# Two fused attention blocks on one core: the first norm's averages one quarter earlier in a weight product, and layer 0's bias products behind the second Q and K

## The chip, the cores and the metric

The kernel runs on one core of one Trainium2 chip. The metric is device time in microseconds (us) of the whole program, median over several executions. The core's engines work side by side, each through its own queue in order: TensorE (PE, matmuls; PEld is its weight load), VectorE (DVE), ScalarE (ACT), GpSimd (POOL), and SyncE (SP), which here issues nearly all DMAs. Line numbers (L504) are those of the kernel as the profile names them.

## The reference, cut to what matters

Input x is (8, 512, 32, 32), float32: 8 samples of 512 channels and 1024 positions. Two attention blocks with residuals follow each other.

```python
# layer 0: group norm (32 groups), 8 heads of 64
h = group_norm(x, norm_w, norm_b)
q, k, v = heads(einsum('oc,bchw->bohw', qkv_w, h) + qkv_b)
attn = softmax(einsum('bhnd,bhmd->bhnm', q, k) / sqrt(64))
o = einsum('bhnm,bhmd->bhnd', attn, v)
x = x + einsum('oc,bchw->bohw', proj_w, o) + proj_b

# layer 1: norm over the whole sample, one head of 512
n = (x - mean) * rsqrt(var + 1e-5) * gn_gamma + gn_beta
q, k, v = wq @ n + bq, wk @ n + bk, wv @ n + bv
attn = softmax(q^T k / sqrt(512))
x = x + wo @ (v attn^T) + bo
```

Since the rows of a softmax sum to one, the bias of V goes through attention unchanged. Layer 0's V bias can therefore be multiplied with the projection weights once (`proj_w @ bv + proj_b`) and be added behind the projection; the kernel does that, and the like for layer 1.

## The kernel before

**Tiling.** A sample is four tiles of 128 partitions x 1024 floats, each tile two channel chunks of one half of the positions. All matmuls are float32, and each shows in the profile as two records. Projections use a Strassen scheme (`strassen`, with seven products in place of eight): its weights come in parts A11, A12, A22 and a rest (A21), and four sums S1 to S4 that `Weight.finish` makes on VectorE (L182 to L185) and then stores to DRAM for the later samples (L220). The data side has the sums T1 to T4 (`Combined.first` and `second`). The products A11 x B11 and A12 x B21 come first and need no sum.

**Order.** TensorE, ScalarE and VectorE run in the order in which the program writes their instructions. `strassen` is a generator that yields between products; `together` interleaves several of them, and `at_steps` counts the yields and runs hooks after given ones. The second Q and K of layer 0 (`pairs_qk(w, 1, ...)`: channel chunks 1 and 3) make ten yields, 0 to 9, even for Q, odd for K. At step 8 Q's last two products (A22 x T4 and S4 x B22) are issued, at step 9 K's. SP's queue is not written by hand: the framework orders its DMAs and hands out the tile buffers.

**Buffers.** Most SBUF tiles (x, q, k, v, p, sums, `many`, `row`) come from one pool of 36. Three weight buffers rotate. PSUM has two tags, "s" and "o", of two buffers each; a buffer is two banks. `strassen` takes one "s" buffer and one "o" buffer, and leaves the second bank of the "o" one as `spare[0]`, in which the small averages of the norms are made (`room`).

**Start of the program.** First come the statistics of sample 0; the product of layer 1's V and output weights (`product(wvo1, ...)`, 16 matmuls of 512 columns); then the product of layer 1's Q and K weights (`wqk1`), in four quarters over `cc` of four matmuls each. `product` runs the callbacks of `between` behind the second and the fourth matmul of its last quarter: `norm.mean_of_all` (a small matmul at L268, then VectorE L272 to L312) and `norm.variance_of_all` (a matmul, VectorE, a power on GpSimd at L318, VectorE L326 to L328). Behind the product come two `Through` objects (bias1 and bias_q1): each copies a column of the vectors to 32-column blocks (`many`, L500, VectorE) and makes four matmuls with 32 weight columns each, one column group per channel chunk (L504). Then `norm.normed` (L336 on ScalarE, L338 on VectorE), `taken` (ScalarE copies of the finished product, L545 and L546), and the first Q and K of layer 0.

**Seam of sample 0.** In `layer0`, after V (L453, done at L485 and L487) the program adds up the two biases, finishes the weights qk13 and p0 and makes `Through` bias0 from p0's parts:

```python
        w = next_weight()
        if b == 0:
            w.finish()
            waiting[0].finish()
            p0 = waiting[0]
            ...
            throughs[:] = [Through(moving, V_BV0, V_BP0, "bias0", banks("s", "ps_bias0")[:, 0, :])]
            throughs[0].store()
            throughs[0].fetch()
```

`store` copies the row on ScalarE (L508) and issues four small DMAs (L511), `fetch` four more (L516); `add`, behind all of layer 0's scores, adds them up. Then the second Q and K run (L438; ScalarE copies L385, VectorE additions L470, ScalarE L468), with the next sample's norm in hooks 4 to 7 and the first scores (`score`, L626) in hooks 8 and 9.

Of the kernel before, what the change touches and what calls it, by code (L numbers as in the profile page):

```python
# [40 lines left out]
P = 128  # L41
C = 512
NC = C // P
# [16 lines left out]
def two_attention_blocks(  # L60
# [17 lines left out]
    nc = tc.nc  # L78
# [13 lines left out]
    def banks(tag, name):  # L92
        return psum.tile([P, 2, HALF], FP, tag=tag, name=name)

    def tile2(name):
        return tpool.tile([P, 2, HALF], FP, tag="t", name=name)
# [93 lines left out]
    class Weight:  # L190
# [3 lines left out]
        def __init__(self, name):  # L194
            self.name, (self.src, self.widths) = name, SOURCES[name]
            self.tile = wpool.tile([P, W_SIZE], FP, tag="w", name=f"w_{name}")
            self.parts, self.rest, at = [], [], 0
            for width in self.widths:
                size = len(A_PARTS) * 2 * width
                self.parts.append(parts_of(self.tile[:, at : at + size], width))  # L200
                at += size
            if name in stored:
                nc.sync.dma_start(self.tile, stored[name])
# [29 lines left out]
    waiting = []  # L233
# [191 lines left out]
    def at_steps(steps, hooks):  # L425

        n = -1
        for n, _ in enumerate(steps):
            for hook in hooks.get(n, []):
                hook()  # L430
        assert n >= max(hooks, default=-1)
# [44 lines left out]
    def make_v(w, n2, bs, vs, name):  # L476
# [11 lines left out]

        return strassen(by_positions(w, n2, bs), done, f"{name}_{n2}")

    class Through:

        def __init__(self, moving, v_bias, bias, name, ps):
            self.bias, self.name, self.ps = bias, name, ps
            many = tile2(f"many_{name}")[:, 0, :P].rearrange("p (c m) -> p c m", c=NC)
            at = vec[:, v_bias : v_bias + NC]
            nc.vector.tensor_copy(many, at.unsqueeze(2).to_broadcast([P, NC, P // NC]))  # L500
            for cc in range(NC):
                for to, w in moving(cc):
                    rows = ps[cc * (P // NC) : (cc + 1) * (P // NC), to]
                    nc.tensor.matmul(rows, many[:, cc, :], w, start=True, stop=True)  # L504
# [23 lines left out]
    def product(w, a, b, tag, between=()):  # L528


        w.rest = [tile2(f"rest_{w.name}")[:, :, : 2 * P]]
        ps = [banks(tag, f"ps_{w.name}_{j}") for j in range(2)]
        between = list(between)
        for cc in range(NC):
            for to in range(NC):
                nc.tensor.matmul(  # L536
                    ps[to // 2][:, to % 2, :], a[cc][:, to * P : (to + 1) * P], b[cc],
                    start=cc == 0, stop=cc == NC - 1,
                )
                if cc == NC - 1 and to % 2 and between:  # L540
                    between.pop(0)()

        def taken():
            for j in range(2):
                nc.scalar.copy(w.parts[0][f"A1{j + 1}"], ps[j][:, :, : 2 * P])  # L545
                nc.scalar.copy(w.parts[0]["A22"] if j else w.rest[0], ps[j][:, :, 2 * P :])  # L546

        return taken
# [49 lines left out]
    def layer0(bs, qs, ks, b, load_next, norm_next):  # L598
# [69 lines left out]
        ps = {}  # L668
# [4 lines left out]
        w = next_weight()  # L673
        if b == 0:
            w.finish()
            waiting[0].finish()
            p0 = waiting[0]

            def moving(cc):
                for i in range(2):  # L680
                    a = p0.rest[0] if (i, cc // 2) == (1, 0) else p0.parts[0][f"A{i + 1}{cc // 2 + 1}"]
                    yield slice(i * 2 * P, (i + 1) * 2 * P), a[:, cc % 2, :]

            throughs[:] = [Through(moving, V_BV0, V_BP0, "bias0", banks("s", "ps_bias0")[:, 0, :])]
            throughs[0].store()
            throughs[0].fetch()
        hooks = {8: [lambda: score(0)], 9: [lambda: score(1)]}
        *pairs, end = ORDER
        if norm_next is not None:
            hooks[4] = [lambda: norm_next().mean_of_all()]  # L690
            hooks[5] = [lambda: norm_next().variance_of_all()]
            combine = Combined(f"0_{b + 1}")
            for half in range(2):
                hooks[6 + half] = [lambda half=half: norm_next().normed(norm_next().xs, [half])]
            hooks[8].insert(0, lambda: combine.first(norm_next().xs))
            hooks[9].insert(0, combine.second)
            bs_next = combine.parts
        at_steps(together(*pairs_qk(w, 1, bs, qs, ks, b)), hooks)
        xs = load_x(b, nc.sync)
        norm = norm1(xs, b)  # L700
# [243 lines left out]
    with tc.manual_schedule(engines={PE, ACT, DVE}):  # L944
        norm = norm0(xs_next, 0)
        for cc in range(NC):
            norm.of_half(cc, 0)
        for cc in range(NC):
            norm.of_half(cc, 1)
            norm.of_channels(cc)  # L950
        wvo1 = Weight("wvo1")
        product(wvo1, nv1, wo1, "o")()
        waiting.append(load_first("qk02"))
        wqk1 = Weight("wqk1")
        wvo1.finish()
        spare[0] = banks("o", "ps_norm")[:, 0, :]
        taken = product(wqk1, nq1, nk1, "s", [norm.mean_of_all, norm.variance_of_all])
        spare[0] = None
        ps = banks("o", "ps_biases")
        everywhere = slice(0, C)  # L960
        throughs += [
            Through(lambda cc: [(everywhere, wo1[cc])], V_BV1, V_BO1, "bias1", ps[:, 0, :]),
            Through(lambda cc: [(everywhere, nk1[cc])], V_BQ1, None, "bias_q1", ps[:, 1, :]),
        ]
        norm.normed(xs_next)
        taken()
        waiting.append(load_first("v0"))
        for through in throughs:
            through.store()
        combine = Combined("0_0")  # L970
        combine.first(xs_next)
        waiting[0].finish()
        combine.second()
        bs = combine.parts
        qs, ks = [None] * NC, [None] * NC
        w = next_weight()
        at_steps(
            together(*pairs_qk(w, 0, bs, qs, ks, 0)), {2: [wqk1.finish], 8: [waiting[0].finish]}
        )
        for through in throughs:  # L980
            through.fetch()
        for b in range(B):
            ahead = []

            def load_next():
                ahead.append(norm0(load_x(b + 1, nc.sync), b + 1))

            norm_next = (lambda: ahead[0]) if b + 1 < B else None
            xs, norm, bs = layer0(bs, qs, ks, b, load_next, norm_next)

            qs, ks = [None] * NC, [None] * NC
            hs, combine = quarters_of(f"h_1_{b}"), Combined(f"1_{b}")
            steps = [
                norm.mean_of_all, norm.variance_of_all, lambda: norm.normed(hs, [0]),
                lambda: norm.normed(hs, [1]), lambda: combine.first(hs), combine.second,
            ]
            if b + 1 < B:
                at_steps(
                    together(*pairs_qk(next_weight(), 0, bs, qs, ks, b + 1)),
                    {n + 4: [step] for n, step in enumerate(steps)},  # L1000
                )
            else:
                for step in steps:
                    step()
            at_values = {}
            if b + 1 < B:

                again, combine_next = ahead[0], Combined(f"again_{b}")

                def load_again():  # L1010
                    again.xs = load_x(b + 1, nc.sync)

                at_values = {
                    2: [load_again], 5: [lambda: again.normed(again.xs, [0])],
                    6: [lambda: again.normed(again.xs, [1])], 8: [lambda: combine_next.first(again.xs)], 9: [combine_next.second],
                }
                bs = combine_next.parts
            attention1(xs, combine.parts, b, at_values)
            for half in range(2):
                for i in range(2):  # L1020
                    nc.sync.dma_start(quarter_of(out, b, i, half), xs[i][half])


        assert next(extents, None) is None
        good = small.tile([P, 1], FP, tag="good", name="good")
        nc.vector.tensor_reduce(good, extent, AX.X, ALU.add)
        nc.vector.tensor_scalar(good, good, MOST, None, ALU.is_le)
        ps = banks("o", "ps_good")[:, 0, :]
        nc.tensor.matmul(ps[:, 0:1], ones, good, start=True, stop=True)
        nc.vector.tensor_copy(flag, ps[0:1, 0:1])  # L1030
# [412 lines left out]
```

## Time and profile before

| | us |
|---|---|
| median of 9 runs | 2953.09 |
| lowest, highest | 2951.51, 2954.72 |
| profiled execution, time | 2953.3 |
| profiled execution, span from first to last instruction | 2951.6 |
| mean granted TensorE clock | 0.995 |
| TensorE busy | 2916.4 |
| VectorE busy | 1753.7 |
| ScalarE busy | 1070.8 |

The profile is one execution of the program. In the timeline a row gives the start, the length, the engine, the line, the operation with its tiles (out<-in, buffer numbers left out), how many instructions are merged in it, and in brackets the idle time of the engine ahead of it with what ended it. "issue" means that no releaser is seen. The lengths of matmuls include their pipeline, so rows overlap a little.

### The profile page before, as it was taken

To read this page: it belongs to the slowest core of one execution; us is meant where nothing else is said; L and a number is where in the kernel's file an instruction comes from. 1 tells how busy PE (TensorE), PEld (TensorE's weight loads), DVE (VectorE), ACT (ScalarE), POOL (GpSimd) and SP (SyncE) were. 2 spreads that over 40 slices of the span, in tenths; PEclk is the share of its full clock that TensorE was granted. 3 is DMA by queue.
4 is the path that set the end of the run, shared out by engine and by line. 5 is a ranking of instruction groups with operands and counts; after the bars stand their busy time and mean duration, and the time that the engine had idled before them with its cause. 6 is when DMAs were issued, how large, how long until landed. Compare 5 with 4: busy or idle time off the path is not lost.

```text
span 2951.6 us, 33920 instructions
## 1 busy us (share of the span) xinstructions
PE 2916.4 (99%) x14018; PEld 1359.1 (46%) x14018; DVE 1753.7 (59%) x2142; ACT 1070.8 (36%) x1512; POOL 13.9 (0%) x26
## 2 busy tenths in 40 slices
PE   9999999999999999999999999999999999999898
PEld 4434545345543455334553354533545335453353
DVE  4577265862658536684366844578445783547835
ACT  2363224622146221562215522165222642226321
POOL 0000000000000000000000000000000000000000
PEclk9999999999999999999999999999999999999999
DMA  7301122011220112202031021310212212120001
GB/s 252 148 15 45 62 66 106 23 50 50 93 79 23 50 50 93 86 15 75 26 118 62 15 75 34 109 62 15 75 61 82 69 33 75 43 91 24 8 0 37
DMA packets 63402, 184.27 MB, mean 62 GB/s; under 512 B 13308, under 2 KB 13820, under 8 KB 56840
## 3 DMA queue, kind: packets, MB, share of 16 engines
q1 hardware_dynamic: 63096, 182.01, 18.0%
q8 instruction: 112, 1.84, 0.3%
q14 instruction: 50, 0.41, 0.0%
q10 hardware_dynamic: 144, 0.02, 0.0%
HBM read 137.41 MB, written 27.81 MB: 56 GB/s over the span
## 4 chain that ended last, share of the span: by engine, by line
PE 95%; DVE 4%; ACT 1%; issue 0%; SPq 0%; DMA 0%; POOL 0%; DVEq 0%; POOLq 0%
PE s L626 15%; PE ps_o L645 14%; PE ps_q L438 13%; PE ps_v L453 13%; PE ps_o L893 13%; PE ps_s L836 13%; PE ps_k L438 7%; PE ps_p L438 4%; DVE inv L566 1%; PE ps_sum L659 1%; DVE acc L555 1%; PE ps_wvo L536 1%; PE ps_wqk L536 0%; DVE t_p L711 0%; DVE t_p L705 0%
## 5 line engine op out<-in xcount | busy, mean ns | idle before, releaser
L553 ACT ACTIVATE p<-s 128x1024 f32<-128x1024 f32 x512 | 523.8, 1025 | 314.7 <-PE s L626 311.3
L626 PE MATMUL s<-q,k 64*64 64x512 f32 x4096 | 532.6, 591 | 0.0
L645 PE MATMUL ps_o<-p,v 64*64 64x512 f32 x4096 | 528.7, 589 | 0.0
L555 DVE TENSOR_TENSOR acc<-acc,p 128x1024 f32<-128x1024 f32 x384 | 468.7, 1220 | 80.7 <-ACT p L553 63.7
L626 PEld LDWEIGHTS s<-q,k 64*64 64x64 f32 x4096 | 151.9, 133 | 295.1 <-issue 254.0
L645 PEld LDWEIGHTS ps_o<-p,v 64*64 64x64 f32 x4096 | 156.6, 133 | 282.8 <-issue 280.3
L844 DVE TENSOR_TENSOR p<-ps_s,u_s 128x512 f32<-128x512 f32 x96 | 66.4, 692 | 249.7 <-ACT u_s L385 139.4
L487 DVE TENSOR_TENSOR v<-ps_v,u_v 128x512 f32<-128x512 f32 x96 | 66.3, 690 | 201.4 <-PE ps_v L453 130.5
L385 ACT COPY u_v<-ps_v 128x512 f32<-128x512 f32 x96 | 56.3, 586 | 326.3 <-PE ps_v L453 320.0
L385 ACT COPY u_q<-ps_q 128x512 f32<-128x512 f32 x96 | 56.3, 586 | 317.5 <-PE ps_q L438 317.4
L836 PE MATMUL ps_s<-s_q,t 128*128 128x512 f32 x384 | 167.4, 592 | 0.0
L893 PE MATMUL ps_o<-t_p,s_v 128*128 128x512 f32 x384 | 166.1, 592 | 0.0
L555 DVE TENSOR_TENSOR acc<-p,p 128x1024 f32<-128x1024 f32 x64 | 78.4, 1225 | 98.9 <-ACT p L553 98.9
L438 PE MATMUL ps_p<-t_p,w_p 128*128 128x512 f32 x256 | 113.3, 595 | 4.5 <-DVE inv L566 4.5
L470 DVE SCALAR_TENSOR_TENSOR q<-ps_q,bias_q,u_q 128x512 f32<-128x512 f32 x48 | 36.0, 751 | 137.2 <-ACT u_q L385 74.8
L836 PEld LDWEIGHTS ps_s<-s_q,t 128*128 128x128 f32 x384 | 73.0, 190 | 91.8 <-issue 91.8
L893 PEld LDWEIGHTS ps_o<-t_p,s_v 128*128 128x128 f32 x384 | 73.0, 190 | 91.8 <-issue 88.5
L893 PE MATMUL ps_o<-p,v 128*128 128x512 f32 x256 | 113.3, 595 | 0.0
L453 PE MATMUL ps_v<-w_wvo,t 128*128 128x256 f32 x512 | 113.1, 379 | 0.0
L836 PE MATMUL ps_s<-q,h 128*128 128x512 f32 x256 | 112.5, 592 | 0.0
L438 PE MATMUL ps_q<-t,w_wqk 128*128 128x512 f32 x256 | 112.5, 592 | 0.0
L566 DVE RECIPROCAL inv<-ps_sum 128x512 f32<-128x512 f32 x32 | 107.4, 3356 | 7.1 <-ACT held_sum L562 7.1
(208 smaller groups left out, 3601.0 us busy)
## 6 DMA issues: line engine op xcount, KB each, us to landing
x<-in_x SPq DMA_DIRECT2D x92, 512.0 KB
w_qk<-stored_qk SPq DMA_DIRECT2D x14, 1792.0 KB
out<-x SPq DMA_DIRECT2D x32, 512.0 KB
w_wqk<-stored_wqk SPq DMA_DIRECT2D x8, 1792.0 KB
w_wvo<-stored_wvo SPq DMA_DIRECT2D x8, 1792.0 KB
w_v<-stored_v SPq DMA_DIRECT2D x7, 1792.0 KB
w_p<-stored_p SPq DMA_DIRECT2D x7, 1792.0 KB
inv<-inv SPq DMA_DIRECT2D x192, 64.0 KB
```

Source lines behind the costliest of these rows:

```text
L385: nc.scalar.copy(us[n], line)
L438: nc.tensor.matmul(bank, w[a][:, k, c * P : (c + 1) * P], bs[b][:, k, :], start=fresh and k == 0, stop=k == 1, skip_group_check=True,)
L453: nc.tensor.matmul(bank[:, u * 2 * P : (u + 1) * 2 * P], bs[b][:, k, n * P : (n + 1) * P], w[a][:, k, :], start=fresh and u == k == 0, sto ...
L487: nc.vector.tensor_tensor(v, pairs(bank), pairs(u), ALU.add)
L553: nc.scalar.activation(p, s, AF.Exp, scale=factor)
L555: nc.vector.tensor_tensor(acc, first, p, ALU.add)
L566: nc.vector.reciprocal(inv, ps)
L626: nc.tensor.matmul(s[cols, j, :], flat(ks[pair])[rows, k0 : k0 + HD], qs[pair][rows, g, :], start=True, stop=True,)
L645: nc.tensor.matmul(o[cols, half, :], vs[kt][rows, c0 : c0 + HD], p[rows, j, :], start=kt == 0, stop=kt == NT - 1,)
L836: nc.tensor.matmul(bank, bs[b][:, k, t * P : (t + 1) * P], q_parts[a][:, k, :], start=fresh and k == 0, stop=k == 1, skip_group_check=True,)
L844: nc.vector.tensor_tensor(p, bank, u, ALU.add)
L893: nc.tensor.matmul(bank, v_parts[kt // 2][a][:, kt % 2, c * P : (c + 1) * P], p_parts[kt // 2][b][:, kt % 2, :], start=fresh and kt == 0, ...
```

## The change

Three things. In `product`, the callbacks run in the last quarter but one (`cc == NC - 2`) in place of the last. The copy to `many` becomes a function of its own, and for bias1 and bias_q1 it is called ahead of the product. For sample 0, `p0.finish` moves into hook 7 of the second Q and K (behind the second half of the next sample's normalisation), and the products, store and fetch of bias0 become the first thing in hook 8, ahead of `combine.first` and of the first scores; the products are written to the spare bank in place of an "s" buffer.

```diff
+    def many(v_bias, name):
+        t = tile2(f"many_{name}")[:, 0, :P].rearrange("p (c m) -> p c m", c=NC)
+        at = vec[:, v_bias : v_bias + NC]
+        nc.vector.tensor_copy(t, at.unsqueeze(2).to_broadcast([P, NC, P // NC]))
+        return t
...
-        def __init__(self, moving, v_bias, bias, name, ps):
+        def __init__(self, moving, many, bias, name, ps):
             self.bias, self.name, self.ps = bias, name, ps
-            many = tile2(f"many_{name}")[:, 0, :P].rearrange("p (c m) -> p c m", c=NC)
-            at = vec[:, v_bias : v_bias + NC]
-            nc.vector.tensor_copy(many, at.unsqueeze(2).to_broadcast([P, NC, P // NC]))
...
-                if cc == NC - 1 and to % 2 and between:
+                if cc == NC - 2 and to % 2 and between:
                     between.pop(0)()
...
         if b == 0:
             w.finish()
-            waiting[0].finish()
             p0 = waiting[0]
...
-            throughs[:] = [Through(moving, V_BV0, V_BP0, "bias0", banks("s", "ps_bias0")[:, 0, :])]
-            throughs[0].store()
-            throughs[0].fetch()
+            def bias0():
+                throughs[:] = [Through(moving, many(V_BV0, "bias0"), V_BP0, "bias0", room("bias0"))]
+                throughs[0].store()
+                throughs[0].fetch()
...
+        if b == 0:
+            hooks.setdefault(7, []).append(p0.finish)
+            hooks[8].insert(0, bias0)
         at_steps(together(*pairs_qk(w, 1, bs, qs, ks, b)), hooks)
...
+        manys = [many(V_BV1, "bias1"), many(V_BQ1, "bias_q1")]
         taken = product(wqk1, nq1, nk1, "s", [norm.mean_of_all, norm.variance_of_all])
...
-            Through(lambda cc: [(everywhere, wo1[cc])], V_BV1, V_BO1, "bias1", ps[:, 0, :]),
-            Through(lambda cc: [(everywhere, nk1[cc])], V_BQ1, None, "bias_q1", ps[:, 1, :]),
+            Through(lambda cc: [(everywhere, wo1[cc])], manys[0], V_BO1, "bias1", ps[:, 0, :]),
+            Through(lambda cc: [(everywhere, nk1[cc])], manys[1], None, "bias_q1", ps[:, 1, :]),
```

## The prediction

> **What bounds the kernel now.** I read the page first, then TensorE's own waits over the whole run, and then the timeline of the two places that those waits point to. The page says that TensorE sets the time:
>
> ```profile
> PE 2916.4 (99%) x14018; PEld 1359.1 (46%) x14018; DVE 1753.7 (59%) x2142; ACT 1070.8 (36%) x1512; POOL 13.9 (0%) x26
> ```
>
> The span is 2951.6 us, so TensorE is idle for about 35 us in all, and an edit that adds or removes no matmul can only gain from these or from a slow clock. The waits of TensorE name where some of them lie (columns: total us, times, longest us):
>
> ```profile
> PE ps_bias L504 <- issue: 7.2, 1, 7.2
> ...
> PE ps_biases L504 <- DVE many_bias_q L500: 2.4, 1, 2.4
> ...
> PE ps_q L438 <- ACT rest_wqk L546: 0.3, 1, 0.3
> ```
>
> All three lie where the change edits. The timeline of the first place (start us, length us, engine, line, what, and the idle time before it):
>
> ```profile
> 33.12 0.28 PE L268 MATMUL ps_norm<-stat,in_group 128*128 128x4 f32 x2
> 35.06 0.28 PE L268 MATMUL ps_norm<-spread,in_group 128*128 128x4 f32 x2
> 35.89 1.01 POOL L318 TENSOR_TENSOR rstd<-rstd,minus_half 128x4 f32<-128x4 f32 x1 [33.88 <-DVE rstd L317]
> 37.53 2.93 ACT L336 ACTIVATE x<-x,shift,scale 128x512 f32<-128x512 f32 x4 [15.16 <-DVE shift L328]
> 37.78 1.94 PE L504 MATMUL ps_biases<-wo,many_bias 128*32 128x512 f32 x8 [2.44 <-DVE many_bias_q L500]
> 41.46 3.70 PE L438 MATMUL ps_q<-x,w_qk 128*128 128x512 f32 x8 [0.32 <-ACT rest_wqk L546]
> ```
>
> The product of layer 1's weights ends with the variance matmul at 35.06. Its answer goes through VectorE, GpSimd and VectorE to the shift, ScalarE normalises from 37.53 (four activations, 2.93 us), and then copies ps_wqk out of the PSUM buffer that the first Q needs (copies at 40.37 and 40.83). So Q starts at 41.46, and what ended last is ScalarE's chain from the shift; the bias products between (37.78 to about 41.1) end just ahead of it. The statistics were ready long before, at 19.4 (aggregate at 19.17 for 0.21).
>
> The second place is the seam between batch 0's V and its second Q and K:
>
> ```profile
> 96.19 0.68 DVE L185 TENSOR_TENSOR w_p<-w_p 128x512 f32<-128x512 f32 x1
> 96.80 0.22 DVE L500 COPY many_bias<-vec 128x128 f32<-128x128 f32 x1
> 97.12 1.10 PE L504 MATMUL ps_bias<-w_p,many_bias 128*32 128x256 f32 x8 [7.18 <-issue]
> ...
> 99.00 5.25 PE L438 MATMUL ps_q<-x,w_qk 128*128 128x512 f32 x8
> ...
> 104.10 3.60 PE L438 MATMUL ps_k<-x,w_qk 128*128 128x512 f32 x8
> ```
>
> V's products end at 89.94 (chain of waits: "65.76 24.17"). TensorE then stands for 7.18 us. The releaser reads "issue", but the first bias product reads `many_bias`, which VectorE writes at 96.80 after the last V addition, five small additions, eight operations of qk13's finish and four of p0's. Behind it, eight records of Q take 5.25 us where K's eight take 3.60: the clock. The granted clock by the microsecond (columns: stretch, sum; PE, PEld, DVE, ACT, POOL busy; PEclk; DMA share; GB/s):
>
> ```profile
> 37.00:38.00 1.00, 0.22 (x4) 0.23 (x8) 0.93 (x6) 0.47 (x1) 0.00 (x0) 0.66 0.00 0
> ...
> 96.00:97.00 1.00, 0.00 (x0) 0.00 (x0) 1.00 (x3) 0.00 (x0) 0.00 (x0) 0.50 1.01 430
> ...
> 103.00:104.00 1.00, 1.00 (x3) 0.38 (x3) 0.00 (x0) 0.17 (x1) 0.00 (x0) 1.00 0.99 416
> ```
>
> **The change, part by part.** All sums are against the profiled execution: span 2951.6 us, time 2953.3, of which 1.7 lies outside the span. The median of the nine runs, 2953.09, is 0.2 below it.
>
> *Averages in the third quarter.* The weight product is 32 records of 0.43 us, 8 to a quarter. The mean matmul follows the 20th record in place of the 28th, the variance the 24th in place of the 32nd: each 8 x 0.43 = 3.43 us earlier, at 29.7 and 31.6. VectorE has been idle since 25.0 (idle of 8.41 before the mean's copy), and needs 1.07 us from the mean matmul to the finished spread (33.12 to 34.19) where 1.9 are there, so neither stalls the product. The shift and ScalarE's start move from 37.53 to 34.10. ScalarE's last-quarter inputs are there: ps_wqk's first buffer is complete about 33.4, its second at 35.3, both before the copies at 36.9. Q moves to 41.46 - 3.43 = 38.03.
>
> *`many` for bias1 and bias_q1 ahead of the product.* Two VectorE copies of 0.22 us go into the idle stretch from 25.0: nothing on the path. The 16 bias products no longer wait for them and follow the product at once, at 35.3. They run in four column groups, four records together: 0.84 us for four at clock 0.50 (37.78 to 41.1), thus 0.43 at full clock, 1.7 us, over at 37.0. They are under the ScalarE chain by 1 us. If they ran at the old pace, 3.36 us, they would end at 38.7 and be the bound; the gain would be 2.8. I take 3.4, since the clock read 1.00 until 37.3 and the array is now busy up to 37.0. **First place: -3.4 (bounds -2.8 and -3.4).** Everything up to the seam follows the Q start and moves along.
>
> *Nothing ahead of the second Q and K.* The bias0 products leave, and with them the wait. The first Q product reads A11 of qk13, which needs no finish, and batch 0's normalised x; DMA share is 0.00 from about 78 to 90, so the weights have landed. Its PSUM buffers are those that V's first half gave back (copy at 84.79, addition at 86.52). Q's eight records end 3.43 us after V, K's eight at 6.86. In old times: 89.94, 93.37, 96.80. VectorE finishes qk13 at 94.3, adds q by 95.0, and Q's S1 product needs both at 96.80: covered by 1.8 us. Gone are 99.08 - 89.94 = 9.14 us, and 5.18 - 3.43 = 1.75 us of half clock in the first Q: -10.9.
>
> *What comes back at the end of the second Q and K.* p0.finish is now in VectorE's queue after the second half of the next sample's normalisation (step 7), and bias0 stands in TensorE's queue between Q's last product and the first scores (step 8). The old rows there:
>
> ```profile
> 119.94 0.99 DVE L338 TENSOR_SCALAR x<-x,scale,shift 128x512 f32<-128x512 f32 x2
> ...
> 121.80 1.09 PE L626 MATMUL s<-q,k 64*64 64x512 f32 x8
> 121.91 0.75 DVE L470 SCALAR_TENSOR_TENSOR q<-ps_q,vec,u_q 128x512 f32<-128x512 f32 x1 [0.98 <-PE ps_q L438]
> ```
>
> VectorE had 0.98 us free before Q's last addition. Now four operations come in at 120.87, and took 96.80 - 94.26 = 2.54 us at the seam: free at 123.4. Then q's addition (0.67 to the next start) and `many` at 124.1; the products start 0.32 after it (96.80 to 97.12), at 124.4. TensorE is there at 121.8: **a new stall of 2.6 us**, with the scores, the rest of K and all else queued behind it. The 16 products of 256 columns took 1.96 us at clock 0.50, thus 1.0 at full clock. ScalarE's row copy (0.59) stands ahead of the first exponential, which waits for the scores anyway; combine.first, 2.4 us on VectorE, is for the next sample and late for nobody: k's last addition follows K's products, some 3.6 us further on. Cost: +3.6.
>
> *DMAs.* The store of p0 (1.79 MB), four stores of 2 KB and four fetches leave the seam, where DMA share was about 1.0, and go on SP's queue after qk13's store and about the load of wqk1 and the reload of x (126.55 and 126.94). Their readers are far: bias0 is added at 242.5, the x reload is read at 253. Bounds 0 and, if a tile has to wait for the row's store, the 8 us from row copy to last fetch at the seam (99.14 to 107.1); I take 0.
>
> *The clock at the new stall* is the open term. The row: at the first place TensorE was idle from 35.3, and the clock fell to half near 37.3, 2.0 us later (0.66 in 37 to 38), though only 2.44 us were idle. At the seam it fell near 95.3, 5.4 us after V. The Trainium skill ("TensorE: Matmul & The Clock Gate", Part 1: The HAM clock gate) says that the array is throttled after at least one idle window of about 3.4 us, that the windows run free, and that a busy one lifts it. By the idle-window rule a stall of 2.6 us costs no clock: the sum is -3.4 - 10.9 + 3.6 = -10.7. By the row of 2.44 us it may: a window of 3.4 us at half speed loses 1.7, and the sum is -9.0. The row overrides the word "idle": a window that was partly busy was enough. But clock edges at 37.3, 40.7, 95.3 and 102.2 fit one grid of 3.41 us, as the page has it. On it the new stall, at 121.8 - 14.3 = 107.5 to 110.1, is cut by an edge at 109.0: the window before it is busy for 1.9 of 3.4 us, against 1.4 in the one that lost the clock. I take full clock, and keep the other end for the range.
>
> **Sum.** -3.4 - 10.9 + 2.6 + 1.0 = -10.7: span 2940.9, time 2942.6 for the profiled execution, 2942.4 for the median. Later stages are paced by TensorE and move along whole.
>
> **The rivals.**
> - *Half clock at the new stall.* For it: the 2.44 us row, and a grid that need not lie alike in each run. Against: the cut at 109.0. 2953.1 - 9.0 = 2944.1.
> - *The stall is covered*, because VectorE runs ahead of what I laid out. Against: its queue is in order and the four operations are 2.54 us. -13.3: 2939.8.
> - *Only one half works.* If Q stays bound in the first place (bias products or the copies late), only the seam's -7.3 is left: 2945.8. If the second Q stays behind VectorE (an operation of the finish that I think it doesn't need), only -3.4: 2949.7, within 0.2% of before.
> - *Slower: a tile buffer held by SP's queue.* The many and row tiles of bias0 now come after the q and k tiles in the pool of 36 that the exponentials' p tiles also come from. SP issues in order; its longest wait for K's products was 24.0 us (load of a weight). If the row's stores are queued behind such a wait and a p tile is given the row's buffer, exponentials and TensorE stand for it. It decides once that wait passes 10.7 us; at 24.0 the result is +13: 2966. For it: an exponential did wait once for a DMA of x (0.7 us). Against: I count about 33 live tiles of 36 there.
>
> **How the numbers follow.** This measurement can tell about 0.2% (5.9 us) from no change. Chances: the sum as taken 0.50; half clock 0.22; stall covered 0.05; seam only 0.07; first place only 0.06; small waits that eat all of it 0.03; the SP wait 0.07. Below 2947.2 lie the first four: faster 0.84. First place only and small waits: same 0.09. Slower 0.07. The range goes from 2939.5 (just under the covered stall) to 2947.0 (past seam only), leaving out about 0.17.
>
> **What would show it.** Mean matmul near 29.7, variance near 31.6, first ScalarE normalisation near 34.1, bias products right behind the product and about 1.7 us in all, Q at about 38.0 with an idle of about 1 us before it. V's last product and Q's first without a gap near 86.5, eight Q records in about 3.6 us, clock 1.00. `ps_bias` products near 110 with about 2.6 us of idle before them, ended by VectorE's `many_bias`, 1.0 us long; longer says half clock. Wrong if TensorE still stands before the second Q, if `ps_q` still starts after 40, or if exponentials of batch 0 show waits for DMAs.

## The result, and the profile after

| | before | changed |
|---|---|---|
| median, us | 2953.09 (30 runs, 2951.33 to 2954.72) | 2943.29 (10 runs, 2942.30 to 2944.35) |
| profiled execution: time, span | 2953.3, 2951.6 | 2941.7, 2940.0 |
| ratio of medians | | 0.9967 (95%: 0.9959 to 0.9975) |

The change saves 9.8 us by the medians, where the prediction had 10.7. In the page, TensorE's busy time falls by 5.3 us although it has the same 14018 matmul records, which is clock and not work:

```profile
PE 2911.1 (99%) x14018; PEld 1357.3 (46%) x14018; DVE 1753.7 (60%) x2142; ACT 1070.7 (36%) x1512; POOL 13.9 (0%) x26
```

TensorE's own waits (total us, times, longest us). The 7.2 us of `ps_bias` are gone, and so are the 2.4 of `ps_biases`. One wait is new. It is that of bias0's products, which now stand in the spare bank of `ps_k`, and it is ended by the copy that the prediction named:

```profile
PE ps_k L508 <- DVE many_bias L495: 2.4, 1, 2.4
...
PE ps_q L438 <- ACT rest_wqk L550: 0.7, 1, 0.7
```

The timeline of the first place in the changed kernel. The averages now stand inside the product, the bias products follow it, and TensorE waits 0.74 us for ScalarE before Q:

```profile
28.82 0.28 PE L268 MATMUL ps_norm<-stat,in_group 128*128 128x4 f32 x2
30.75 0.28 PE L268 MATMUL ps_norm<-spread,in_group 128*128 128x4 f32 x2
33.23 2.93 ACT L336 ACTIVATE x<-x,shift,scale 128x512 f32<-128x512 f32 x4 [11.73 <-DVE shift L328]
34.51 1.06 PE L508 MATMUL ps_biases<-wo,many_bias 128*32 128x512 f32 x8
37.16 3.70 PE L438 MATMUL ps_q<-x,w_qk 128*128 128x512 f32 x8 [0.74 <-ACT rest_wqk L550]
```

The seam and the end of the second Q and K: V's last product, Q right behind it, then VectorE's finish and the late `many`, and the stall in front of bias0's products:

```profile
83.75 1.89 PE L453 MATMUL ps_v<-w_v,x 128*128 128x256 f32 x8
85.48 3.60 PE L438 MATMUL ps_q<-x,w_qk 128*128 128x512 f32 x8
...
107.59 0.69 DVE L185 TENSOR_TENSOR w_p<-w_p 128x512 f32<-128x512 f32 x1
108.19 0.75 DVE L470 SCALAR_TENSOR_TENSOR q<-ps_q,vec,u_q 128x512 f32<-128x512 f32 x1
...
108.85 0.22 DVE L495 COPY many_bias<-vec 128x128 f32<-128x128 f32 x1
...
109.12 0.66 PE L508 MATMUL ps_k<-w_p,many_bias 128*32 128x256 f32 x8 [2.44 <-DVE many_bias L495]
...
110.15 1.09 PE L630 MATMUL s<-q,k 64*64 64x512 f32 x8
```

And the granted clock there (columns as in the prediction; the clock is the third number from the end). It stays full behind the stall in this execution:

```profile
108.00:109.00 1.00, 0.00 (x0) 0.00 (x0) 1.00 (x4) 0.00 (x0) 0.00 (x0) 1.00 0.00 0
109.00:110.00 1.00, 0.88 (x16) 0.49 (x16) 1.00 (x2) 0.00 (x0) 0.00 (x0) 1.00 1.07 459
```

The two profiles add up stage by stage. The marks are TensorE's first Q, its second Q (before: 99.00 with 9.14 of seam ahead of it), the first scores, and the first Q of sample 1 (266.75 before, 255.09 after):

| stage, us | before | changed | difference | predicted |
|---|---|---|---|---|
| start to first Q | 41.46 | 37.16 | -4.30 | -3.4 |
| first Q to second Q | 57.54 | 48.32 | -9.22 | -9.1 |
| second Q to first scores | 22.80 | 24.67 | +1.87 | +1.8 |
| first scores to sample 1 | 144.95 | 144.94 | -0.01 | 0 |
| rest, to the end of the span | 2684.85 | 2684.91 | +0.06 | 0 |

The first row has 0.87 too much, and it lies ahead of the change: the second weight product starts at 20.23 in place of 21.10. Measured from there, Q comes 3.43 earlier (20.36 to 16.93), the figure of the prediction. That start varies by itself: over the profiles of this study, with the same work ahead of it, it lies between 19.80 and 21.39. To the end of the span, measured from that start, are 2930.5 us before and 2919.8 changed: -10.7.

### The profile page after: what moved, and what is told of

Read it like the earlier page. It is cut to its first block, busy times and chain, and to the rows that moved or that the text cites. A ratio compares the mean times of both kernels' runs of the same rounds, so it can differ in the third digit from the quotient of the medians.

```text
span 2940.0 us, 33922 instructions
## 1 busy us (share of the span) xinstructions
PE 2911.1 (99%) x14018; PEld 1357.3 (46%) x14018; DVE 1753.7 (60%) x2142; ACT 1070.7 (36%) x1512; POOL 13.9 (0%) x26
## 4 chain that ended last, share of the span: by engine, by line
PE 95%; DVE 4%; ACT 1%; issue 0%; DMA 0%; SPq 0%; POOL 0%; DVEq 0%; POOLq 0%
PE s L630 15%; PE ps_o L649 14%; PE ps_v L453 13%; PE ps_o L901 13%; PE ps_q L438 13%; PE ps_s L844 13%; PE ps_k L438 7%; PE ps_p L438 4%; DVE inv L570 1%; PE ps_sum L663 1%; DVE acc L559 1%; PE ps_wvo L540 1%; PE ps_wqk L540 0%; DVE t_p L719 0%; DVE t_p L713 0%; ACT p L557 0%
## 5 line engine op out<-in xcount | busy, mean ns | idle before, releaser
L630 PE MATMUL s<-q,k 64*64 64x512 f32 x4096 | 532.6, 591 | 0.0
L630 PEld LDWEIGHTS s<-q,k 64*64 64x64 f32 x4096 | 151.9, 133 | 294.7 <-issue 254.4
```

What stands on the lines that cost most here:

```text
L630: nc.tensor.matmul(s[cols, j, :], flat(ks[pair])[rows, k0 : k0 + HD], qs[pair][rows, g, :], start=True, stop=True,)
```

## The experiments

The medians are in us. Each ratio is to runs of the kernel before on the same chip, whose medians are 2952.84 (e1 to e4), 2953.35 (e5 to e8) and 2953.55 (e9 to e12). The changed kernel was measured twice, with medians of 2943.29 and, in e10, 2942.02; a difference of 1.3 us between two medians therefore says nothing by itself. What an edit does is read from the profiles, between two marks around both places: the start of the second weight product, and the second scores (the row `s<-q,k` with x16 at L630, or L626 before the change). The last column is what lies behind the second mark. No edit touches it, and yet it spans 1.7 us.

| run | median | ratio to before (95%) | product's start to second scores | second scores to end of span |
|---|---|---|---|---|
| before | 2953.09 | | 105.35 | 2825.1 |
| changed | 2943.29 | 0.9967 (0.9959 to 0.9975) | 94.57 | 2825.2 |
| e1_first_only | 2949.72 | 0.9989 (0.9983 to 0.9996) | 101.99 | 2825.1 |
| e2_seam_only | 2946.10 | 0.9977 (0.9969 to 0.9986) | 97.99 | 2825.7 |
| e3_finish_in_3 | 2939.41 | 0.9955 (0.9942 to 0.9969) | 92.05 | 2825.0 |
| e4_finish_twice | 2947.10 | 0.9982 (0.9975 to 0.9988) | 98.50 | 2825.0 |
| e5_many_late | 2943.53 | 0.9970 (0.9958 to 0.9981) | 94.57 | 2826.1 |
| e6_many_early_only | 2949.11 | 0.9985 (0.9979 to 0.9992) | 101.13 | 2826.4 |
| e7_second_quarter | 2941.22 | 0.9963 (0.9949 to 0.9976) | 93.75 | 2825.6 |
| e8_both | 2938.08 | 0.9952 (0.9939 to 0.9966) | 91.25 | 2825.1 |
| e9_filled | 2943.32 | 0.9970 (0.9958 to 0.9981) | 94.63 | 2825.9 |
| e10_changed_again | 2942.02 | 0.9962 (0.9948 to 0.9975) | 94.57 | 2825.9 |
| e11_finish_in_3_many_in_8 | 2940.59 | 0.9957 (0.9943 to 0.9971) | 93.11 | 2825.7 |
| e12_finish_at_seam | 2940.83 | 0.9959 (0.9945 to 0.9972) | 93.11 | 2824.7 |

**e1 and e2: each place alone.** e1 is the changed kernel with bias0 back at the seam:

```diff
             w.finish()
+            waiting[0].finish()
             p0 = waiting[0]
...
-            def bias0():
-                throughs[:] = [Through(moving, many(V_BV0, "bias0"), V_BP0, "bias0", room("bias0"))]
+            throughs[:] = [Through(moving, many(V_BV0, "bias0"), V_BP0, "bias0", banks("s", "ps_bias0")[:, 0, :])]
...
-        if b == 0:
-            hooks.setdefault(7, []).append(p0.finish)
-            hooks[8].insert(0, bias0)
```

> Only the first place is changed (averages in the third quarter, the two early copies); bias0 stays at the seam as before. If the gains of the two places add up, Q starts 3.4 us earlier against the end of the weight product and the seam keeps its 9.1 us and its half clock: 2953.1 - 3.4 = 2949.7 against before. If the two places share one wait further on, so that either alone earns nothing (a later DMA or VectorE chain takes it back), the time is that of before, 2953.

e2 is the changed kernel with the start of before:

```diff
-                if cc == NC - 2 and to % 2 and between:
+                if cc == NC - 1 and to % 2 and between:
...
-        manys = [many(V_BV1, "bias1"), many(V_BQ1, "bias_q1")]
         taken = product(wqk1, nq1, nk1, "s", [norm.mean_of_all, norm.variance_of_all])
+        manys = [many(V_BV1, "bias1"), many(V_BQ1, "bias_q1")]
```

> Only the seam is changed (p0's finish in hook 7, bias0 in hook 8); the start is as before. If the gains add up: 9.1 us of seam and 1.8 us of half clock go, 2.4 us of stall and 1.0 us of products come, thus -7.4 or 2945.7. If the start's gain is needed for it, less than that. In the profile Q follows V without a gap, and the products of bias0 stand 2.4 us behind Q's last.

Measured: -3.1 and -6.7 by the medians, each against before on the same chip, and -3.36 and -7.36 between the marks. The two add up to -9.8 and -10.72; both at once bring -9.8 and -10.78. The places are independent. e1 keeps the whole of the old seam, the wait and the slow Q behind it:

```profile
93.54 1.10 PE L508 MATMUL ps_bias<-w_p,many_bias 128*32 128x256 f32 x8 [7.17 <-issue]
...
95.42 5.33 PE L438 MATMUL ps_q<-x,w_qk 128*128 128x512 f32 x8
```

e2 has the old start, and shows which of its waits counted. The bias products wait for the same 2.44 us as before, but in this profile they run at full clock and end earlier. Q gains nothing by it: TensorE waits longer for ScalarE, and Q starts 20.36 us behind the start of the weight product (20.70), as it did before (21.10 to 41.46). So it was ScalarE's chain that held Q, and the half clock of the bias products cost nothing:

```profile
37.38 1.07 PE L508 MATMUL ps_biases<-wo,many_bias 128*32 128x512 f32 x8 [2.44 <-DVE many_bias_q L495]
...
41.06 3.70 PE L438 MATMUL ps_q<-x,w_qk 128*128 128x512 f32 x8 [1.76 <-ACT rest_wqk L550]
```

**e5 and e6: which of the two edits at the first place.** e5 makes only the second part of e2's edit (the copies late, the averages still early), e6 only its first part (the averages late, the copies still early).

> The changed kernel with the copies to many_bias1 and many_bias_q1 made behind the weight product again (behind the shift in VectorE's queue); the averages stay in the third quarter. If the early averages alone made the gain of the first place: the copies come at about 33.2, before the product ends at 34.5, the bias products still follow at once, and the time is that of the changed kernel within 0.3 us. If the early copies were what freed the bias products and these were the bound, Q starts later by up to 2.4 us: 2945.7.

> The changed kernel with the averages back in the last quarter; the two copies stay early. If ScalarE's chain from the shift sets Q's start, the bias products follow the weight product at once at full clock and TensorE then waits about 4.5 us for Q: +3.4 against the changed kernel, near 2946.7. If the bias products were the bound, most of the gain stays: near 2943.5 to 2944.

e5 is the changed kernel: 2943.53, and the same 94.57 us between the marks. Its copies come at 34.00 and 34.13 on VectorE, the product ends at 35.35, and the bias products follow at once and leave the same 0.74 us before Q:

```profile
35.39 1.06 PE L508 MATMUL ps_biases<-wo,many_bias 128*32 128x512 f32 x8
...
38.05 3.70 PE L438 MATMUL ps_q<-x,w_qk 128*128 128x512 f32 x8 [0.74 <-ACT rest_wqk L550]
```

So the early copies are worth nothing once the averages are early. e6 went as expected in kind and further in size: 2949.11 where 2946.7 stood. The bias products follow the product, TensorE waits 4.27 us for ScalarE's chain, and Q itself then runs at half clock:

```profile
41.76 5.19 PE L438 MATMUL ps_q<-x,w_qk 128*128 128x512 f32 x8 [4.27 <-ACT rest_wqk L550]
```

Eight records take 5.19 us here, and 3.70 in e5. The early copies alone put the bias products right behind the product, and one long idle stretch stands ahead of Q in place of two short ones. In the kernel before, the clock was at half under the bias products and full again near 40.7, ahead of Q. Between the marks e6 is 6.56 us longer than the changed kernel: 3.44 for Q's later start, 1.5 for Q's half clock, and 1.65 at the stall further on, which is shown below. Its profiled execution (2950.62) is also the slowest of its 21 runs, so the median has less of this.

**e3, e11 and e12: what the new stall is made of.** e3:

```diff
         if b == 0:
-            hooks.setdefault(7, []).append(p0.finish)
+            made_many = []
+            hooks.setdefault(3, []).extend([p0.finish, lambda: made_many.append(many(V_BV0, "bias0"))])
             hooks[8].insert(0, bias0)
```

> The changed kernel with p0's finish and the copy to many_bias0 in hook 3 in place of hooks 7 and 8. If the stall at step 8 is VectorE's four finish operations and the copy behind q's last addition, nothing is left of it: -2.4 us against the changed kernel, near 2940.9, and TensorE goes from Q's last product to bias0's without a wait. If the products wait there for something else (the PSUM bank that the norm's averages used, a weight part), the stall of 2.4 us stays and the time is 2943.3.

e11 moves only `p0.finish` to hook 3 and leaves `many` in hook 8:

```diff
-            hooks.setdefault(7, []).append(p0.finish)
+            hooks.setdefault(3, []).append(p0.finish)
```

> The changed kernel with p0's finish in hook 3, the copy to many_bias0 left in hook 8. If the copy's place behind q's last addition matters by itself, a stall of about 1.1 us stays (addition 0.67, copy to product 0.32, and the wait for Q's product): 1.3 us better than the changed kernel by the stall's length. If only the four finish operations made the stall, nothing is left of it, -2.4.

e12 is e3 with `p0.finish` at the seam, ahead of the second Q and K:

```diff
             w.finish()
+            waiting[0].finish()
             p0 = waiting[0]
...
-            hooks.setdefault(7, []).append(p0.finish)
+            made_many = []
+            hooks.setdefault(3, []).extend([lambda: made_many.append(many(V_BV0, "bias0"))])
```

> The changed kernel with p0's finish back at the seam, behind qk13's and ahead of the second Q and K on VectorE, the copy to many_bias0 in hook 3 and the products in hook 8. If q's first addition had 1.8 us of cover there, the 2.5 us of finish overrun it: Q's S1 product waits about 0.9 us (addition from 92.5 to 93.2 where TensorE wants it at 92.3), and bias0's products wait for nothing: 1.5 us better than the changed kernel by the stalls' lengths. If the cover is larger than 2.5, -2.4; if the first Q products themselves wait for the finish, a stall of several us before Q and a time near or above the changed kernel's.

In e3 the stall is gone: bias0's products stand 1.80 us behind the start of Q's last four records, without an idle time. In e11 0.98 us of it stay, ended by the same copy, and in e12 TensorE waits 0.79 us at Q's S1 product and nowhere at bias0. The rows of e3, e11 and e12 in turn:

```profile
105.41 1.88 PE L438 MATMUL ps_q<-x,w_qk 128*128 128x512 f32 x4
...
107.21 0.66 PE L508 MATMUL ps_k<-w_p,many_bias 128*32 128x256 f32 x8
```

```profile
107.49 0.66 PE L508 MATMUL ps_k<-w_p,many_bias 128*32 128x256 f32 x8 [0.98 <-DVE many_bias L495]
```

```profile
94.39 1.98 PE L438 MATMUL ps_q<-t,w_qk 128*128 128x512 f32 x4 [0.79 <-DVE q L470]
```

So the 2.44 us are 1.46 of finish and 0.98 of a copy that stands behind q's last addition; that addition cannot start until Q's last product is done. e12 measures the cover at the seam: 2.54 us of VectorE work overrun it by 0.79, so it was 1.75 us, where the prediction had 1.8. Between the marks e11 and e12 are each 1.46 us shorter than the changed kernel, and e3 is 2.52 shorter, where 1.3, 1.5 and 2.4 were expected. The medians say the same less sharply: e11 and e12 lie 1.4 and 1.2 us below e10 on the same chip, e3 3.9 below 2943.29 and 2.6 below 2942.02.

**e4, e9 and e10: the clock at the stall.** e4 lengthens the stall by four VectorE operations:

```diff
-            hooks.setdefault(7, []).append(p0.finish)
+            hooks.setdefault(7, []).append(lambda: finish(p0.parts[0], p0.rest[0]))
+            hooks[7].append(p0.finish)
```

> The changed kernel with p0's four sums computed twice in hook 7, so that the stall at step 8 grows by the 2.5 us of four more VectorE operations, from 2.4 to about 5.0 us. If a stall costs its length and no clock: +2.5, near 2945.8, granted clock 1.00 behind it. If a window of 3.4 us that was mostly idle halves the clock, bias0's products take 2.0 in place of 1.0 us and the records behind them 0.85 in place of 0.43 for up to 3.4 us: +3.5 to +4.2, near 2947.

The stall is 4.96 us, and the clock falls. bias0's products take 1.89 us to the first scores in place of 1.03, and the stretch to the next scores 5.20 in place of 4.65: 1.4 us more than the stall. Between the marks e4 is 3.93 us longer, and its median is 3.8 us above 2943.29 and 5.1 above 2942.02, so the half-clock reading holds. Its rows, and one of its clock:

```profile
112.00 1.11 PE L508 MATMUL ps_k<-w_p,many_bias 128*32 128x256 f32 x8 [4.96 <-DVE many_bias L495]
113.89 1.64 PE L630 MATMUL s<-q,k 64*64 64x512 f32 x8
...
119.09 1.95 PE L630 MATMUL s<-q,k 64*64 64x512 f32 x16
```

```profile
113.00:114.00 1.00, 1.00 (x16) 0.19 (x12) 0.90 (x2) 0.00 (x0) 0.00 (x0) 0.50 1.11 459
```

e6 has the changed kernel's own stall of 2.43 us, and its profile shows the half clock behind it, from 116.5 to 119.9, in the first scores and K's products. The clock by the microsecond in e6:

```profile
116.00:117.00 1.00, 1.00 (x16) 0.21 (x8) 0.90 (x2) 0.59 (x1) 0.00 (x0) 0.73 1.11 459
117.00:118.00 1.00, 1.00 (x9) 0.05 (x1) 0.60 (x1) 0.00 (x0) 0.00 (x0) 0.50 0.91 387
...
119.00:120.00 1.00, 1.00 (x3) 0.48 (x2) 0.00 (x0) 0.09 (x1) 0.00 (x0) 0.56 0.49 188
```

From the first to the second scores it has 6.30 us in place of 4.65, thus 1.65 lost. Since e3's median seemed to earn 1.5 us more than the stall's length, e9 tested whether this is common in the timed runs. It fills the stall with matmuls that are overwritten unread:

```diff
+                ps = room("bias0")
+                for _ in range(3):
+                    nc.tensor.matmul(
+                        ps, ones, flat(ks[0])[:, :HALF], start=True, stop=True,
+                    )
-                throughs[:] = [Through(moving, many(V_BV0, "bias0"), V_BP0, "bias0", room("bias0"))]
+                throughs[:] = [Through(moving, many(V_BV0, "bias0"), V_BP0, "bias0", ps)]
```

> The changed kernel with three matmuls of 512 columns (2.6 us of TensorE at full clock, their result overwritten unread) put ahead of bias0's products, into the stall of 2.4 us that VectorE makes there. If the stall costs its length alone, this is the changed kernel, +0.2 us. If the stall also halves the clock behind it in many of the timed executions (which would explain that removing it earned 3.9 us in place of 2.4), the busy array keeps its clock and the median falls by 1 to 1.5 us, against the changed kernel run on the same chip.

> The changed kernel once more, for the same chip and a second profile: 2943.3. If the clock behind the stall depends on where the clock's windows fall, this profile may show bias0's products or the first scores at half clock (up to 1.7 us longer to the first scores) where the first profile showed 1.00. If the clock never falls behind 2.4 us of idle, it shows 1.00 again.

e9 came to 2943.32 and e10, the changed kernel on the same chip, to 2942.02: filling the stall earned nothing (94.63 and 94.57 us between the marks). e10's profile shows the stall of 2.44 us and clock 1.00 behind it once more. So do those of e2, e5 and e7, which have the same stall; e6 is the only one of six in which the clock fell. The half clock behind this stall is thus seen once in six profiles, and nothing shows that it made e3's surplus. That surplus is not in e3's profile, whose gain between the marks is the stall's length; it is of the size by which the changed kernel's own medians differ.

**e7 and e8: the rest of the first place, and a better version.** e7 puts the averages a quarter earlier still, and e8 adds e3's edit:

```diff
-                if cc == NC - 2 and to % 2 and between:
+                if cc == NC - 3 and to % 2 and between:
```

> The changed kernel with the averages in the second quarter of the weight product. If ScalarE's chain still sets Q's start by the 0.74 us that TensorE waits before it, this wait goes and no more: -0.7, near 2942.6, Q right behind the bias products. If Q is bound by the end of the weight product itself through the copies of its result (about 1.1 us for the first buffer), the wait stays and the time is 2943.3.

> Second quarter for the averages and hook 3 for p0's finish and the copy to many_bias0. If the two waits are separate: -0.7 - 2.4 = -3.1 against the changed kernel, near 2940.2. If a later wait takes one back, no better than the better of the two alone.

In both the wait before Q is gone; Q follows the bias products. In e8 neither of the two places has an idle time left:

```profile
34.27 1.06 PE L508 MATMUL ps_biases<-wo,many_bias 128*32 128x512 f32 x8
...
36.13 3.70 PE L438 MATMUL ps_q<-x,w_qk 128*128 128x512 f32 x8
...
105.58 0.66 PE L508 MATMUL ps_k<-w_p,many_bias 128*32 128x256 f32 x8
```

From the start of the bias products to Q it is 1.85 us in e7 and 2.65 in the changed kernel: 0.8 less, where 0.7 was expected, and between the marks it is 0.82 less. e8 is the fastest kernel of the study: 2938.08, which is 5.2 below 2943.29, and 3.32 less between the marks, where 3.1 was expected and e3 and e7 add up to 3.34.

## Why the prediction was right

**The first place.** The working held: each average 8 records earlier, ScalarE's chain from the shift sets Q, the bias products run at full clock under it. From the product's start Q moved by 3.43 us. That ScalarE was the bound, and not the bias products, e2 shows as well. The prediction listed "the 16 bias products no longer wait for them" as if the early copies did it. e5 shows that the early averages do that by themselves. It cost the copies at nothing, and that was right; e6 shows what they would do alone.

**The seam.** Q's first products need nothing from the finish, as said. V to Q has no gap, and eight Q records take 3.60 us in place of 5.25: -9.22 and the clock, against -9.14 and 1.75. The cover of 1.8 us for q's addition was measured by e12 as 1.75.

**What came back.** A stall of 2.6 us was said and is 2.44; 1.0 us for the products, and it is 1.03. The chain was as said: four operations, then q's addition, then `many`, in VectorE's order. What the working did not say is that without the four operations a part would stay. e11 shows it: 0.98 us, because `many` is queued behind an addition that waits for Q's last product.

**The clock at the stall.** This was the open term, with full clock taken. Both profiles of the changed kernel show full clock, and the reason given, that an edge of a window cuts the stall, can be traced. All steps of the clock in one profile lie on one grid: in the kernel before, 95.34 and 2788.46 are 789 windows of 3.413 us apart, and in e6 the half clock lasts from 116.47 to 119.88, one window. (A step is read from the rows of one microsecond: 0.73 in 116 to 117 means full clock until 116.46.) The grid lies elsewhere in each profile, so the same stall is cut elsewhere. In e10 an edge at 109.17, which is 782 windows ahead of its step at 2778.39, cuts the stall of 107.54 to 109.98 almost where the prediction had it (109.0), and no window has more than 1.64 us of idle. In the first profile of the changed kernel the edge lies at 107.25 (783 windows ahead of its step at 2779.88), and the window behind it has 1.88. In e6 the window from 113.05 to 116.47 has 2.14, and the clock fell.

In all fourteen profiles, each window that began at full clock and had 2.02 us of idle or more ended at half clock, and each with 1.93 or less kept full clock (the nearest on either side are in e2 and e4, near 2780 us). Of three with 1.98 or 1.99 us one lost it, the one at the first place before the change. The margin of the first profile was thus about 0.1 us, and the full clock there was in part luck. The Trainium skill ("TensorE: Matmul & The Clock Gate", Part 1: The HAM clock gate) has the array throttled after at least one idle window of about 3.4 us; here a window that was idle for about 2 of its 3.4 us was enough. Its free-running windows fit.

**The rivals.** Half clock: seen in e6 only. The stall was not covered; neither half failed (e1, e2). SP's queue held nothing up: in the changed kernel's timeline the row's four stores start 0.6 us after the row copy begins, and from the first scores to sample 1 both kernels take the same 144.9 us.

**The median.** It moved by 9.8 us and not 10.7. The shortfall is not in the two places: between the marks the profiles differ by 10.78, and behind them by 0.1. The profiled execution (2941.7) lies below all ten timed runs (2942.30 to 2944.35), in part by its early start. e10's median is 11.5 below its own before, on one chip. No run separates the 0.9 us from this spread.

## What to carry to other kernels

When one engine is busy for 99% of the span, list that engine's own waits, longest first, and ask of each what its next instruction truly needs; a short side product in the queue can hold up work that needs nothing of it. Before a piece of work is moved behind another, look at the queue of the engine that prepares its inputs: here the products moved well, and the two small steps that feed them (the finish and the copy) belonged earlier still, which was worth another 2.5 us (e3). Split an edit of several parts: one part of this one was worth nothing beside the other, and alone it cost 1.5 us of clock in the profile taken (e6). When an effect of 1 us is looked for, measure it between two marks close around the edit: here the rest of the program varied by more than that from run to run.

## What the runs showed of the hardware

An idle stretch of TensorE can cost more than its length, and how much depends on where the windows of 3.41 us cut it. The stall of 2.43 to 2.44 us at step 8 cost nothing more in five profiles and 1.65 us more in a sixth. At the first place the same 2.44 us halved the clock before the change (eight records of the bias products in 1.94 us) and left it full in e2 (1.07).

The program's start has a like spread. The first matmul waits for its weights until 4.3 to 4.6 us, and then the records start 0.86 us apart, later 0.43. The pace changes at 7.6 us in e7 and at 10.7 in e6, and the second weight product starts at 19.80 and 21.39: the extremes of the fourteen profiles, as far apart as some of the effects that were looked for. Near 2780 us, in the last sample, all fourteen show half clock again, for 6.8 us in eight of them and for 10.2 in six. That is a part of the spread in the last column: from the same row of `ps_p` (2769.72, and 2770.67 in e10) to the end of the span, the changed kernel with 6.8 us of it takes 170.3 us and e10 with 10.2 takes 170.9.

Where the bias products stood decided Q's clock. Before the change a stall of 2.44 us stood ahead of them; they ran at half clock themselves, and it was full again near 40.7, ahead of Q at 41.46. In e6 they came first, and the 4.27 us of idle behind them held one whole window (37.96 to 41.37): Q ran at half clock.
